# Attention units of a four-layer graph kernel: six of eight cover one head over all nodes instead of two heads over half of them

## The chip, the core and the metric

The kernel runs on one core of one Trainium2 chip. The core has a matrix engine (TensorE, PE in the profile; its weight loads are shown as PEld), a vector engine (VectorE, DVE), a scalar engine (ScalarE, ACT), a general engine (GpSimd, POOL) and SyncE (SP), which issues most of the DMA transfers; POOL and ACT issue some as well. Each engine works through its own list of instructions in order and waits for others by semaphores. SBUF is the on-chip memory of 128 partitions, PSUM the memory that PE writes to. The metric is the device time of one execution in microseconds (us); lower is better.

## What is computed

A graph of N = 3327 nodes has features x (3327 x 512) and a 0/1 adjacency. Four layers follow one another, each x = layernorm(x + layer(x)). Layers 0 and 2 are graph attention with 8 heads of 64 features, layer 3 with 4 heads of 128, layer 1 takes the mean over the first 64 neighbours of a node. Cut to what matters here:

```
# layers 0 and 2: H = 8 heads, D = 64 (layer 3: 4 heads, D = 128)
Wh = x @ W                          # (N, H, D)
f1, f2 = Wh . a1, Wh . a2           # one number a node and head each
e  = leaky_relu(f1[i] + f2[j], 0.2)
e  = where(adj[i, j] > 0, e, -9e15)
att = softmax(e, over j)
h[i] = sum_j att[i, j] * Wh[j]      # layer 2 and 3: then elu
# layer 1
keep = first 64 neighbours of each row
x = leaky_relu(mean(keep) @ W_nb.T + b_nb) + leaky_relu(x @ W_line.T + b_line)
```

## The kernel before

**Tiles.** The nodes are padded to NP = 3328 = 26 tiles of 128 (NT = 26). A half is 13 tiles, IW = 1664 nodes. The mask (adjacency, transposed: neighbours j on the partitions, nodes i along the row) is held as bytes (fp8).

**A unit of attention.** `attention` (L598) runs eight units, `for half in range(2): for s in range(NS)`, and `unit` (L370) does one: a slot s, which is two heads (HS = 2) in layers 0 and 2 and one head in layer 3, for one half of the nodes i. Its loop `for j in range(NT)` (L419) goes over the 26 tiles of neighbours. For each j and each head, `weights` (L408) issues one instruction on DVE, L411, which makes the masked weight `t` (128 x 1664, f32) from the broadcast row `rb` of that head, a column `qc` and the mask, and one on ACT, L414, which makes `y`, its share below the kink of the leaky relu, as bytes. PE multiplies `t` by the values `vj` into four PSUM banks `po` (L434); the two heads of 64 features stand side by side in the array. An f32 matmul shows as two instructions, so one j is 16 `po` matmuls. The sums of the denominator go to `pd` (L386) in `den` (L383): 8 matmuls a j with `y` and the columns `sden`, and 8 with the mask and the columns `sm`. `den` is called for a pair of j at a time, two to three j late (L437); the `sm` part of a pair belongs to one of the four slots of a half (L396), which add to the same `pd`.

**Buffers.** `t` has 6 buffers of one head and half, `y` 7 (layer 0) or 8, `vj` 4 of two tiles of 128 features, `rb` 3 rows (2 in layer 3). The rows of a unit are loaded by `rows` (L361) on POOL's queue when a buffer is free; they come out of the DRAM tensor `rd`, which `prepare` (L305) writes.

**Around the loop.** What else has to be done is put into two lists, `background` and `aside`, of which each j takes one job (L439 to L442). At a unit's end ACT copies `po` to `ob` (L454), PE transposes it in four jobs (L462) and SP stores it to `hd`. After the last unit of a half, the sums are finished: by 26 tiny matmuls and `reciprocals` (L561 to L579) after the first half, by DVE transposes and small transfers after the second.

**The mask.** `mask_steps` (L643) loads int32 pieces of the adjacency (`raw`, 128 x 832) and turns each to bytes on DVE (L640) or ACT (L639). The first half's 52 pieces come during the projection of layer 0, the second half's 52 in `aside` during units 0 and 1, one a j, with two `raw` buffers; half 1 of the nodes is first used in unit 4. `count_jobs` (L659) count neighbours, for one half in unit 0, for the other in unit 2. In unit 3 the mask is stored to DRAM (`md`). For layers 2 and 3 `MaskTiles` (L692) loads it back in pieces of a tile and a half: 8 tiles of the first half late in layer 1 on POOL's queue, the others in units 0 and 1 of layer 2 on SP's.

**Order.** PE's order is that of the program; the order of the other engines is decided by a scheduler when the kernel is built, except for instructions that `keep_in_program_order` pins (among them the mask pieces of layer 0's units). `prepare` for the first half is called in layer 0 during its projection (L1186), in layer 1 in one go after tile 12 has been projected (`job2`, L928), where PE works at the sums L908; for the second half it is a job of unit 0.

Of the kernel before, what the change touches and what calls it, by code (L numbers as in the profile page):

```python
# [32 lines left out]
def kernel(  # L33
# [198 lines left out]
    class Layer:  # L232
# [72 lines left out]
        def prepare(self, pool, half, tag="rr", bufs=2, pinned=False):  # L305
# [4 lines left out]
            ins = nc.vector.tensor_scalar(rc, rc, RCLAMP, -RCLAMP, op0=ALU.min, op1=ALU.max)  # L310
            if pinned:
                tc.keep_in_program_order(ins)
            nc.scalar.activation(rc, rc, AF.Exp, scale=ALPHA - 1.0)
            for s0, n in QUADS:
                t0 = half * HALF + s0
                pr = qp.tile([P, 4 * P], F32, name="pr", tag="q")
                for s in range(n):
# [4 lines left out]
            nc.scalar.activation(qc, qc, AF.Exp, scale=1.0 - ALPHA)  # L322

            nc.vector.tensor_scalar(sc.bitcast(I32), qc.bitcast(I32), 0x7F800000, None,
                                    op0=ALU.bitwise_and)
            nc.vector.reciprocal(sc, sc)
            nc.vector.tensor_scalar(sc, sc, STEP, None, op0=ALU.mult)
            nc.vector.scalar_tensor_tensor(bi, qc, -1.0, sc, op0=ALU.mult, op1=ALU.mult)
# [32 lines left out]
        def rows(self, rp, half, s):  # L361
            rb = []
            for h in range(s * self.HS, (s + 1) * self.HS):
                r_ = rp.tile([P, IW], F32, name="rb")
                nc.gpsimd.dma_start(out=r_, in_=self.rd[h:h + 1, half * IW:(half + 1) * IW].to_broadcast([P, IW]))  # L365
                rb.append(r_)
            return rb


# [251 lines left out]
    QW = IW // 2  # L621

    def mask_load(pool, t, q, eng):
# [8 lines left out]
    def mask_set(raw, t, q, on_act=False):  # L632
# [26 lines left out]
    def count_jobs(pool, half):  # L659
        jobs = []  # L660
        for s0, n in QUADS:
# [12 lines left out]
            def none(i0=i0, w_=w_, held=held):  # L674
                ct = pool.tile([P, 4 * P], BF, name="ct", bufs=1)
# [5 lines left out]
                nb = pool.tile([P, 4 * P], F8, name="nb", bufs=1)  # L681
# [10 lines left out]
    class MaskTiles:  # L692
        FIRST = 8
# [5 lines left out]
        def start(self):  # L699
            self.early = self.pools.enter_context(tc.tile_pool(name="mk_a", bufs=1, side="right", reuse_waits="tile"))  # L700

        def load(self, pool, j, half, eng=nc.sync):
            m = pool.tile([P, IW], F8, name=f"mk{half}_{j}")
            ins = eng.dma_start(out=m, in_=md[j * P:(j + 1) * P, half * IW:(half + 1) * IW])
            if eng is nc.sync:
                tc.keep_in_program_order(ins)
            self.tiles[j, half] = m
# [582 lines left out]
```

## Time and profile before

| | us |
|---|---|
| median of 3 runs | 3255.55 (3254.47 to 3257.07) |
| the profiled execution | 3259.11 |
| its span | 3257.0 |
| PE busy | 3137.8 (96%) |
| DVE busy | 2654.7 (82%) |
| ACT busy | 2349.7 (72%) |
| granted PE clock, mean | 0.984 |

Layer 0 projects until some 134 us and its units run until 957; layer 1 runs to some 1600; the units of layer 2 go from 1631 to 2424, and layer 3 ends at 3257. The costliest groups of the page are `po` (L434: 8320 instructions, 1913.4 us), `y` on ACT (L414: 1040, 1770.1) and `t` on DVE (L411: 624 with the mask tiles `mk`, 1180.7, and 416 with `mask`, 779.9).

Busy times on PE are modelled at their ends: a busy PE need not be at its peak. "Idle before" is what the engine waited for just ahead of an instruction. The chain of waits follows the work that ended last back from the end of the program; each of its lines has the start, the length, the engine, the tensor, the line and how many instructions are merged.

### The profile page before, as it was taken

Reading aid. Unit: us, or ns where it says so; the run is one execution under the profiler, and the core shown is the slowest. Engines: PE = TensorE matmul, PEld = TensorE weight load, DVE = VectorE, ACT = ScalarE, POOL = GpSimd, SP = SyncE. Lnnn points to the kernel's source line nnn. Section 1 sums busy time; section 2 is a strip of 40 time slices with the busy share of each in tenths; the row PEclk is TensorE's granted clock in tenths of the full one; section 3 lists DMA queues with packets and bytes.
Section 4 is the critical chain, followed back from the end, with each engine's and each line's share of the span. In section 5 each row is a group of like instructions: output and inputs, shape, how many; then the busy total and the mean of one; then the engine's idle time right before and its main releaser. Section 6 shows DMA issues by size and latency. Waiting matters only on the chain.

```text
span 3257.0 us, 45993 instructions
## 1 busy us (share of the span) xinstructions
PE 3137.8 (96%) x17802; PEld 1670.4 (51%) x17802; DVE 2654.7 (82%) x2581; ACT 2349.7 (72%) x2131; POOL 242.6 (7%) x397
## 2 busy tenths in 40 slices
PE   8899999999999999999989999999998999999997
PEld 7644444444444467767734444444447654445443
DVE  5699999999977645545499999999989666678986
ACT  1398999999973334444389999999988655559976
POOL 3100000000001011111100000000011000010110
PEclk9999999999999999999999999999999999999998
DMA  9445314111124345545412211111127211122211
GB/s 372 158 129 162 102 56 159 46 50 50 46 85 152 102 125 133 140 121 131 133 49 76 82 53 47 36 49 50 43 90 246 90 43 43 42 52 89 94 39 50
DMA packets 337289, 310.63 MB, mean 95 GB/s; under 512 B 154084, under 2 KB 269102, under 8 KB 337071
## 3 DMA queue, kind: packets, MB, share of 16 engines
q1 hardware_dynamic: 302831, 195.34, 20.1%
q0 software_dynamic: 28720, 104.67, 10.1%
q10 hardware_dynamic: 5520, 7.69, 0.7%
q8 instruction: 141, 2.31, 0.3%
q14 instruction: 77, 0.63, 0.1%
HBM read 230.75 MB, written 76.84 MB: 94 GB/s over the span
## 4 chain that ended last, share of the span: by engine, by line
PE 84%; DVE 6%; DMA 4%; ACT 3%; issue 2%; SPq 0%; POOL 0%; ACTq 0%; DVEq 0%; POOLq 0%
PE po L434 53%; PE acc L908 9%; PE pd L386 7%; PE pw L277 5%; DVE t L411 3%; PE pz L807 2%; PE pi L810 2%; DMA raw<-in_adjT_dram 2%; ACT y L414 2%; PE pk L778 1%; PE pt L462 1%; DMA h<-hd 1%; PE pa L1161 0%; DVE xr L197 0%; DVE st L153 0%
## 5 line engine op out<-in xcount | busy, mean ns | idle before, releaser
L414 ACT ACTIVATE y<-t,bi,sc 128x1664 fp8e4<-128x1664 f32 x1040 | 1770.1, 1766 | 308.7 <-PE pd L386 290.6
L434 PE MATMUL po<-t,vj 128*64 128x448 f32 (+3 forms) x8320 | 1913.4, 521 | 23.5 <-DVE t L411 21.2
L434 PEld LDWEIGHTS po<-t,vj 128*64 128x64 f32 (+1 forms) x8320 | 837.9, 148 | 976.2 <-issue 706.9
L411 DVE SCALAR_TENSOR_TENSOR t<-rb,qc,mk 128x1664 f32<-128x1664 f32 x624 | 1180.7, 1939 | 165.6 <-PE po L434 148.8
L411 DVE SCALAR_TENSOR_TENSOR t<-rb,qc,mask 128x1664 f32<-128x1664 f32 x416 | 779.9, 1945 | 8.8 <-PE po L434 5.7
L908 PE MATMUL acc<-zs,kt 128*128 128x512 f32 x1352 | 361.1, 421 | 0.0
L277 PE MATMUL pw<-wsb,xT 128*128 128x264 f32 (+1 forms) x1248 | 299.7, 395 | 10.8 <-ACT xT L268 3.5
L908 PEld LDWEIGHTS acc<-zs,kt 128*128 128x128 f32 x1352 | 257.4, 190 | 52.7 <-PE pk L760 0.8
L386 PE MATMUL pd<-y,sden 128*32 128x448 fp8e4 (+1 forms) x4160 | 259.5, 341 | 11.0 <-ACT y L414 11.0
L767 ACT CAST pk<-cy 128x512 f32<-128x512 bf16 x169 | 99.3, 588 | 236.2 <-DVE kt L781 229.7
L277 PEld LDWEIGHTS pw<-wsb,xT 128*128 128x128 f32 x1248 | 239.7, 196 | 53.5 <-ACT xT L268 8.2
L781 DVE SCALAR_TENSOR_TENSOR kt<-pk,mb 128x512 fp32r<-128x512 f32 x169 | 115.6, 684 | 125.0 <-PE pk L778 123.9
L386 PEld LDWEIGHTS <-sden 128*32 128x32 bf16 x4160 | 117.3, 96 | 163.6 <-issue 140.7
L365 POOL DMA_DIRECT2D rb<-r x40 | 21.5, 537 | 1643.4 <-DVE t L411 1525.7
L283 DVE TENSOR_TENSOR vt<-pw,dc 128x256 f32<-128x256 f32 x156 | 58.8, 416 | 91.3 <-ACT dc L278 87.5
L737 POOL DMA_DIRECT2D cy<-ctd x91 | 68.0, 748 | 392.1 <-ACT pk L767 301.5
L807 PE MATMUL pz<-wn,xT 128*128 128x512 f32 x208 | 95.0, 600 | 0.6 <-ACT xT L801 0.5
L810 PE MATMUL pi<-wl,xT 128*128 128x512 f32 x208 | 93.6, 592 | 0.0
L155 ACT ACT_TABLE_LOAD x46 | 59.0, 1283 | 41.7 <-DVE mv L154 41.1
L182 DVE TENSOR_TENSOR h<-h,rec 128x512 f32<-128x512 f32 x65 | 43.7, 683 | 54.7 <-DMA h<-hd 54.6
L281 ACT COPY rc<-pw 128x8 f32<-128x8 f32 (+1 forms) x78 | 12.7, 162 | 89.3 <-PE pw L277 86.6
L640 DVE TENSOR_SCALAR mask<-raw 128x832 fp8e4<-128x832 int32 (+3 forms) x81 | 49.2, 615 | 25.5 <-DMA raw<-in_adjT_dram 25.4
(185 smaller groups left out, 1650.5 us busy)
## 6 DMA issues: line engine op xcount, KB each, us to landing
vj<-v SPq DMA_DIRECT2D x312, 128.0 KB
rb<-r POOLq DMA_DIRECT2D x40, 832.0 KB, 4.8
raw<-in_adjT_dram SPq DMA_DIRECT2D x67, 416.0 KB
cy<-ctd POOLq DMA_DIRECT2D x78, 256.0 KB, 4.1
h<-hd SPq DMA_DIRECT2D x61, 256.0 KB
v<-vt SPq DMA_DIRECT2D x50, 256.0 KB
hd<-hb SPq DMA_DIRECT2D x48, 256.0 KB
xr<-x POOLq DMA_DIRECT2D x45, 256.0 KB, 3.1
```

What stands on the lines that cost most here:

```text
L155: nc.scalar.activation(rs[:, :n, 0], mv[:, :n, 1], AF.Sqrt, bias=eps)
L277: nc.tensor.matmul(pw[e][:, :FW + H], xT[:, c, :], wsb[:, c, e, :], start=c == 0, stop=c == FC - 1)
L386: nc.tensor.matmul(pd[c][32 * kk:32 * kk + 32, :w_], lhsT, rhs, start=(kk, c) not in seen, skip_group_check=final is not None, stop=last a ...
L411: nc.vector.scalar_tensor_tensor(t, rb[k], self.qc[:, j, h:h + 1], mask_at[0](j, i0, IW), op0=ALU.max, op1=ALU.mult)
L414: nc.scalar.activation(y, t, AF.Sigmoid, bias=self.bi[:, j, h:h + 1], scale=self.sc[:, j, h:h + 1], saturate=False)
L434: nc.tensor.matmul(po[c][k * D:(k + 1) * D, :z - a_], vj[:, j % 2, k * D:(k + 1) * D], ts[k][:, a_:z], start=j == 0, stop=j == NT - 1)
L737: nc.gpsimd.dma_start(out=cy[:, :n, :], in_=ctd[t:t + n, b * GW:(b + 1) * GW] .rearrange("(o t) i -> o t i", o=1).to_broadcast([P, n, GW]))
L767: nc.scalar.copy(pks[k % 2], carry[b, t // 4 * 4][:, t % 4:t % 4 + 2, :])
L781: nc.vector.scalar_tensor_tensor(kt, pk, NEIGHBOURS, mb[:, t:t + 2, :], op0=ALU.is_le, op1=ALU.mult)
L807: nc.tensor.matmul(pz, xT[:, c, :], wn[:, c, :], start=c == 0, stop=c == FC - 1)
L810: nc.tensor.matmul(pi, xT[:, c, :], wl[:, c, :], start=c == 0, stop=c == FC - 1)
L908: nc.tensor.matmul(acc, kts[b, t][:, s * P:(s + 1) * P], zs(t, c), start=t == 0 and c == 0, stop=t == NT - 1 and c == 1)
```

## The change

Layers 0 and 2 get units of their own (`unit8`, `attention8`). Layer 3 keeps `unit`. The eight units are now: unit 0, heads 0 and 1 over the first half ("narrow", as before); six "wide" units, of one head each over all 3328 nodes, in two groups of three (heads 2, 4, 6, then 3, 5, 7); unit 7, heads 0 and 1 over the second half. A wide unit makes `t` and `y` of a j with one instruction each over 3328 elements; PE's matmuls have the shapes they had, with the two halves where the two heads were. Each group has its own `pd`.

```diff
+    UNITS = [Unit(0, 0, 1, half=0, head=0)] + \
+        [Unit(1 + par, n, 3, head=2 * slot + par) for par in range(2) for n, slot in enumerate((1, 2, 3))] + \
+        [Unit(3, 0, 1, half=1, head=0)]
...
+        def den(j, y):
...
+            order = [(c, k, e) for c in range(2) for k in range(2) for e in range(2)]
+            if j % u.of == u.pos:
+                for c, k, e in order:
+                    a_, w_ = part(c, e)
+                    x_ = 32 * u.section(k)
+                    go(c, k, e, self.sm[:, j, x_:x_ + 32], mask_at[0](j, u.base(k) + a_, w_), w_, False)
+            for c, k, e in order:
+                a_, w_ = part(c, e)
+                x_ = 88 * u.section(k) + PIECES[u.slot] - 8 * u.slot
+                go(c, k, e, self.sden[:, j, x_:x_ + 32], y[:, k, a_:a_ + w_], w_, u.last)
+
+        def weights(j, t, y, k):
+            if u.wide:
+                h, to, yo, ro, m = u.h, *(a.rearrange("p k i -> p (k i)") for a in (t, y, rb)), mask_at[0](j, 0, NP)
+            else:
+                h, to, yo, ro, m = u.h + k, t[:, k, :], y[:, k, :], rb[:, k, :], mask_at[0](j, u.base(k), IW)
+            nc.vector.scalar_tensor_tensor(to, ro, self.qc[:, j, h:h + 1], m, op0=ALU.max, op1=ALU.mult)
+            nc.scalar.activation(yo, to, AF.Sigmoid, bias=self.bi[:, j, h:h + 1],
+                                 scale=self.sc[:, j, h:h + 1], saturate=False)
...
+            for c, (a_, z) in enumerate(CUTS):
+                for k in range(2):
+                    x_ = 0 if u.wide else k * D
+                    nc.tensor.matmul(po[c][k * D:(k + 1) * D, :z - a_], vj[:, j % 2, x_:x_ + D],
+                                     t[:, k, a_:z], start=j == 0, stop=j == NT - 1)
+            late.append((j, y))
+            while len(late) > 1 + (n == 0 and j < 2):
+                den(*late.pop(0))
...
+            for k in range(2 if u.wide else 1):
+                w_ = D if u.wide else 2 * D
+                r0 = u.base(k) + s0 * P
+                nc.sync.dma_start(out=hd[r0:r0 + n_ * P, f0:f0 + w_].rearrange("(t p) f -> p t f", p=P),
+                                  in_=hb[:, :n_, k * w_:(k + 1) * w_])
...
+        with tc.tile_pool(name="at_t", bufs=3, reuse_waits="tile") as tp, \
+                tc.tile_pool(name="at_y", bufs=3, reuse_waits="tile") as yp, \
+                tc.tile_pool(name="at_v", bufs=3, reuse_waits="tile") as vp, \
```

The buffers of `t` and `y` now hold a j for both halves or heads, three of each. The row of a unit has a ring of two buffers of 3328 (`wide_rows`), one of which stays on for layer 3, whose rows use its two halves. The sums of the first three groups are finished by the tiny matmuls, those of unit 7 by DVE and transfers.

Because unit 1 needs the mask of all nodes, the second half comes earlier and in smaller pieces, and its count follows in unit 1 instead of 2; the attention vectors of layers 2 and 3 are projected in unit 2 instead of 1. In layer 2 the mask tiles of both halves are loaded in unit 0.

```diff
-        pieces = pieces[EARLY:]
+        pieces = [(t, q, IW // 4) for t in range(NT) for q in range(4, 8)]
+        rest = ExitStack()
+        rawp = rest.enter_context(tc.tile_pool(name="raw", bufs=3))
+        ring.insert(0, (rest.enter_context(tc.tile_pool(name="at_s0", bufs=1, reuse_waits="tile")), "rbb"))
+        msteps = mask_steps(rawp, pieces, 2, [k for k in range(len(pieces)) if k % 9 in (1, 3, 5, 7)], True)
+
+        def some(n):
+            for f in msteps[n:n + 3]:
+                f()
...
+                def reload(j):
+                    if j + mask_tiles.FIRST < NT:
+                        mask_tiles.load(j + mask_tiles.FIRST, 0)
+                    mask_tiles.load(j, 1)
```

`MaskTiles.FIRST` goes from 8 to 3. `prepare` is cut into six steps, and layer 1 runs one of them at tile 14 of each following row of sums, instead of all at once:

```diff
+            return [clamp] + [lambda s0=s0, n=n: quad(s0, n) for s0, n in QUADS] + [scales]
...
+                            if side and t == 14:
+                                side.pop(0)()
...
-                                nxt.prepare(sp, 0, "xi", 1)
+                                side.extend(nxt.prepare_steps(sp, 0, "xT", 1))
...
                     if b == len(blocks) - 2:
-                        mask_tiles.load_first()
+                        for j in range(mask_tiles.FIRST):
+                            mask_tiles.load(j, 0, nc.gpsimd)
+                        nxt.first_rows = nxt.wide_rows(ring, UNITS[0])
```

## The prediction

> **What bounds the kernel now.** I read the busy time by stage first, then the chain of waits inside one attention unit, then the timeline of VectorE (DVE) there, and last the chain around `prepare` in layer 1. The columns of the first view are: stretch, its length, then busy us of PE, PEld, DVE, ACT and POOL with their instruction counts, granted clock, DMA share, GB/s.
>
> ```profile
> 751.00:848.00 97.00, 95.50 (x685) 40.50 (x685) 97.00 (x53) 90.33 (x61) 1.06 (x2) 1.00 0.14 45
> ```
>
> This is one unit of layer 0. DVE is busy in all of it, PE in 98%, at full clock. Both look like the bound, so the chain inside the unit has to tell.
>
> ```profile
> 780.54 2.94 PE po L434 x16
> 783.49 0.59 PE pt L462 x4
> 784.07 2.94 PE po L434 x16
> 787.02 1.62 PE pd L386 x27
> 788.64 2.94 PE po L434 x16
> 791.58 0.26 PE pt L462
> 791.84 2.94 PE po L434 x16
> 794.79 0.87 PE pd L386 x14
> 795.65 5.74 PE po L434 x32
> 801.39 0.87 PE pd L386 x14
> 802.26 6.34 PE po L434 x32
> ```
>
> One `po` block is one tile j: 2.94 us when other work stands on both sides, 5.74 for two in a row. A `pd` block of 16 matmuls takes 0.87, of 32 (16 more with `sm`) 1.62, so 16 `sm` matmuls cost 0.75. From 802.26 on the same 32 `po` matmuls take 6.34 and then 6.58: PE has caught up and waits inside the block for `t`. The DVE timeline has the pace of `t`:
>
> ```profile
> 788.70 18.70 DVE L411 SCALAR_TENSOR_TENSOR t<-rb,qc,mask 128x1664 f32<-128x1664 f32 x10
> ```
>
> One instruction lasts 1.94, so the step from one to the next is (18.70 - 1.94)/9 = 1.862 us, and 52 of them make 96.8 us. PE's own work in a unit is 13 x (5.74 + 0.87) + 13/4 x 0.75 + three blocks of transposes of 0.59, one of 0.26 and their breaks 0.5 = 90.8. The markers of the chain at 468.08, 565.69, 663.82, 760.27 and 857.13 put a unit at 97.3: DVE sets the pace, PE has 6 us to spare, ACT 7.
>
> **The wide instruction.** Two rows give DVE's price per element.
>
> ```profile
> L283 DVE TENSOR_TENSOR vt<-pw,dc 128x256 f32<-128x256 f32 x156 | 58.8, 416 | 91.3 <-ACT dc L278 87.5
> L182 DVE TENSOR_TENSOR h<-h,rec 128x512 f32<-128x512 f32 x65 | 43.7, 683 | 54.7 <-DMA h<-hd 54.6
> ```
>
> (683 - 416)/256 = 1.043 ns an element, so 1664 elements are 1.735 us and 0.127 of the step is fixed. A wide instruction takes 3.470 + 0.127 = 3.597 instead of 3.724, and a wide unit 26 x 3.597 = 93.5 of DVE. No row has 3328 elements: it costs at most two old steps (3.724) and at least the elements alone (3.470); I take 3.597. ACT falls too and has room.
>
> **What PE gets in exchange.** `den` runs after each j, no longer after each pair: 26 blocks of 8 matmuls and 26 `po` blocks of 2.94. Layer 3 has such a block of 8 in its chain (two records are missing from the count):
>
> ```profile
> 2877.64 0.49 PE pd L386 x6
> ```
>
> The `sm` matmuls were shared out over the four units of a half, 16 for each fourth pair. Now a group has one unit (narrow) or three (wide), so a narrow unit issues 8 for every j (0.375) and a wide one for every third: over a layer 832 instead of 416. PE's own time:
> narrow 26 x (2.94 + 0.49 + 0.375) + 2.0 = 100.9; wide 26 x 3.43 + 26/3 x 0.375 + 2.0 = 94.4.
> So PE becomes the bound in both: a wide unit is worth 97.3 - 94.4 = 2.9 at best, and a narrow one loses 4. Because PE and DVE (93.5) lie within 1% of each other and the tiles are uneven (3.43 or 3.81), I add 0.7 of waits to each unit: 95.1 and 101.6. The bounds are 0 and the whole 2.9. At a unit's end PE waited for the last `y` (1.76 at 757.92); now one `den` of 8 waits and DVE runs ahead, so I charge nothing more; without that lead it would be 1.8 a unit.
>
> **Side work, no longer hidden.** While DVE set the pace, PE's 6 us hid the counts (four of 1.62 + 0.32 = 7.8 a half), the projection of the attention vectors (8 x 1.0) and the sums (26 tiny matmuls, 1.6). Where PE is the bound they count.
>
> Layer 0, from the first `t` (134.27) to the last `pd` (956.76), 822.5 before. Unit 0 stays with DVE: 96.8 + the mask pieces + 3.8 of counts + 5.4 for cutting the columns of the other half + 2 of starting waits. The second half of the mask is now needed in unit 1, so it comes in 104 pieces of 416 columns, three a j: 76 of them in unit 0, 42 on DVE. An 832-column piece steps in 0.50; a half one lies between 0.25 and 0.50; with the fixed 0.127 it is 0.31, so 13.0. Unit 0: 121.0. PE's 100.9 + 7.8 + 3 hide beneath it. Units 1 to 7: 95.1 + 7.8 + 1.6 = 104.5; 95.1 + 8.0 = 103.1; 95.1; 95.1 + 1.6 = 96.7; 95.1; 95.1; 101.6 + 1.6 = 103.2. With 3.6 for the first wide `t` that PE must await and 0.5 for the last `den`: 817.9, a gain of 4.6.
>
> Layer 2: PE is the bound from 1671.3 on, with 20 tiles of unit 0 left: 20 x 3.81 + 0.5 = 76.7, then 96.7, 95.1, 95.1, 96.7, 95.1, 95.1, 103.2: it ends at 2425.0 against 2424.0 (2422.24 + 1.79), a loss of 1.0. The mask tiles come two a j on SP's queue instead of one; they are asked for three tiles ahead, some 11 us, and the 208 KB are less than the raw piece below, so nothing. The 26 loads of the second half stood in unit 1's list before; they are moved, not added.
>
> **The mask pieces' loads.** Three buffers, and a load waits for the third piece before it. Behind a waiting load stand the `vj` loads on SP's queue, which have three pairs of lead, and behind a late piece, pinned in DVE's order, the next `t`. In the old stretch:
>
> ```profile
> 263.66 4.20 DMA raw<-in_adjT_dram
> 970.20 1.94 DMA mb<-md
> ```
>
> 416 KB took 4.20 and 64 KB 1.94, so 208 KB should land in about 2.9. The ring turns in 2.9 + 0.35 (issue) + 0.31 (set) + 0.9 until the engine's turn (half a step of `t`) = 4.5, and a j of unit 0 has 121/26 = 4.65. That is hardly enough; I charge 4 us. Lower bound 0, or -3 if the wait on the last old piece (7.86 at 357.22) is no longer there; upper bound with 4.20 for the half piece: (5.76 - 4.65) x 35 = 39.
>
> The wide units' `vj` and `hd` rows are 256 bytes instead of 512. The `mb` transfer above is 64 KB in rows of 256 bytes, as a wide `vj` is: 1.94, with 7.2 us for each and three buffers, so nothing. The Trainium skill (DMA: Bandwidth & Descriptors, Specifications) speaks against the change here: below 512 bytes a transfer loses line rate. By that rule a wide `vj` would take as long as a narrow one with twice the bytes; it would still be hidden, and the sum would stay as it is.
>
> **Rows prepared in six places** (layer 1, bounded by PE).
>
> ```profile
> 1404.57 1.28 ACT L313
> ...
> 1410.83 1.82 DMA r<-rr
> ...
> 1413.37 0.38 PE pr L318
> 1413.75 3.41 PE acc L908 x8
> ```
>
> PE leaves its projection at 1404.37 and is back at its sums at 1413.75: 9.4 us, in which 13 transposes do 2.0 of work. They waited for the table load and Exp, for `qc` and for one buffer `rr` whose store came late. Split over six rows of tiles (35 us apart) each store is long done: 7.4 gained (bounds 0 and 9.4). The `rr` now shares the buffer of `xT`, free between tiles 9 and 21 when the step runs at 14; were it not, PE would wait for a 1.8 us store.
>
> The rest (rows in a ring of two, one `e` buffer at the layer's end, layer 3's rows in one tile) moves transfers that were issued 92 us early; 0, bounds -1 and +2.
>
> **Sum:** -4.6 + 1.0 + 4 - 7.4 = -7.0. The profiled execution has a span of 3257.0 (3259.11 in all); the median of the runs is 3255.55. 3255.55 - 7.0 = 3248.5.
>
> **Rivals.**
> 1. No waits: PE's bare sums hold (0.7 less in 14 units, 9.8) and the pieces come in time (4): 3234.7. For it: PE ran exactly at 2.94 and 0.87 from 760 to 802. Against it: DVE is only 1% below. Chance 0.20.
> 2. Slower: unit 0 waits for raw pieces. It decides from a landing above 3.0 us. At 3.8 the ring takes 5.36, 0.71 more than a j has, over 35 j 25 us instead of 4: 3269.5. For it: three pieces of 213,000 bytes in 4.65 are 137 GB/s, on top of the rest, where one of 426,000 came in some 4.0. Against it: 256 KB of `xr` land in 2.9 by the median of its issues. Chance 0.20.
> 3. The wide instruction saves nothing (3.724): DVE holds a wide unit at 96.8 + 0.7, 2.4 more in 12 units: 3277. Against it: the two rows above. Chance 0.10.
> 4. Slower: splitting `pd` costs more than 0.49 a block. At 0.60, 0.11 x 26 x 14 = 40: 3288; it decides from 0.51. Against it: the block of 8 in layer 3. Chance 0.07.
>
> **How the numbers follow.** The forecast has 0.43, its own range 3238 to 3258. What a measurement can tell from no change is about 0.2%, 6.5 us. Faster: rival 1 and a little over half of the forecast, 0.43; same: most of the rest and the mild ends of 2 and 3, 0.20; slower 0.37. The range goes from 3228 (rival 1 with the whole 9.4 in layer 1, the old last-piece wait gone, 3, and the rest at -1) to 3282 (past rival 3, short of rival 4).
>
> **What would show it.** In a wide unit `t` steps in 3.60 and the span of a unit is 94.4 to 96, with DVE showing idle time that `po` ends; in a narrow one about 101, with `sm` in every `den`. If `po` still shows blocks stretched by `t`, DVE is still the bound. Idle time of DVE before a mask piece, ended by the raw load, would be rival 2. No idle time of PE before `pr` in layer 1 would confirm the 7.4. The forecast is wrong if wide units stay at 97 or unit 0 takes over 130.

## The result and the profile after

The changed kernel takes 3267.74 us (median of 7 runs, 3263.78 to 3275.56) against 3255.38 for the kernel before: a ratio of 1.0039, with a 95% interval of 1.0027 to 1.0051. It is slower, by 9 to 17 us. The forecast was 3248.5, faster by 7. The profiled execution took 3265.22 with a span of 3263.5; that is 2.5 below its median, and the profiled execution of before was 3.7 above its own, so the two traces differ by 6.5 us only. Stage by stage (each mark is the start of the first, or the end of the last, instruction named):

| stage | before | after | difference | predicted |
|---|---|---|---|---|
| start to last `pd` of layer 0 | 956.9 | 958.0 | +1.1 | -0.6 (-4.6 and +4 for raw pieces) |
| to first `po` of layer 2 | 675.9 | 668.9 | -7.0 | -7.4 |
| to last `pd` of layer 2 | 791.3 | 794.8 | +3.5 | +1.0 |
| to first `po` of layer 3 (its projection) | 134.4 | 141.9 | +7.5 | 0 |
| to the end | 698.6 | 699.9 | +1.3 | 0 |

First the wide units, by the busy time in one of them, unit 5 of layer 0 (columns: stretch, its length, then busy us of PE, PEld, DVE, ACT and POOL with counts, granted clock, DMA share, GB/s):

```profile
663.00:757.70 94.70, 94.70 (x723) 35.16 (x716) 93.82 (x27) 85.13 (x36) 1.05 (x2) 1.00 0.13 37
```

94.7 instead of 97.3, PE now busy in all of it and DVE a little less. The timeline of PE inside unit 4 (start, length, engine, line, operation, count) shows why:

```profile
571.43 3.01 PE L717 MATMUL po<-t,vj 128*64 128x448 f32 x16
574.37 0.56 PE L675 MATMUL pd<-y,sden 128*32 128x448 fp8e4 x8
574.86 3.01 PE L717 MATMUL po<-t,vj 128*64 128x448 f32 x16
577.80 0.56 PE L675 MATMUL pd<-y,sden 128*32 128x448 fp8e4 x8
578.29 3.01 PE L717 MATMUL po<-t,vj 128*64 128x448 f32 x16
581.24 0.56 PE L675 MATMUL pd<-mask,sm 128*32 128x448 fp8e4 x8
581.58 0.60 PE L675 MATMUL pd<-y,sden 128*32 128x384 fp8e4 x8
582.11 3.01 PE L717 MATMUL po<-t,vj 128*64 128x448 f32 x16
```

From one `po` to the next it is 3.43 (574.86 - 571.43), and 3.82 where `sm` comes between (582.11 - 578.29). No line of this stretch has idle time in front. The timeline of DVE in the same unit has thirteen wide instructions in a row:

```profile
557.42 46.83 DVE L695 SCALAR_TENSOR_TENSOR t<-rba,qc,mask 128x3328 f32<-128x3328 f32 x13
```

One lasts 3.68, so a step is (46.83 - 3.68)/12 = 3.596. In layer 1, PE's timeline has the row transposes, now in four of the six places, some 17.7 us apart, with no wait in front of any:

```profile
1425.69 0.60 PE L324 MATMUL pr<-ident,rc 128*8 128x128 f32 x4
1443.46 0.60 PE L324 MATMUL pr<-ident,rc 128*8 128x128 f32 x4
1460.99 0.60 PE L324 MATMUL pr<-ident,rc 128*8 128x128 f32 x4
1478.75 0.28 PE L324 MATMUL pr<-ident,rc 128*8 128x128 f32 x1
```

Unit by unit, from the first `po` of a unit to the first of the next (of the last to its last `pd`), the six wide units of layer 2 are 14.9 us shorter together (570.1 against 585.0), and the two narrow ones 18.2 longer (118.7 and 105.9 against 108.7 and 97.7). Layer 0 has the same picture: 10.8 shorter and 13.7 longer.

One pair of traces is not enough to price these two layers. In the seven traces that have the new units with `den` at each j (this one and those of later runs, some with edits of buffers or of the mask's pieces), layer 2 took 794.8 to 802.0, in the four with the old units 788.7 to 791.3; layer 0 ended at 954.4 to 962.7 against 953.1 to 956.9.

The largest new loss is in layer 3's projection, where the rows of layer 3 are prepared in one go. PE's timeline there, before and after (in square brackets the idle time ahead of an instruction and what ended it):

```profile
2503.79 1.04 PE L318 MATMUL pr<-ident,rc 128*4 128x128 f32 x8 [0.90 <-ACT rc L281]
2506.04 0.75 PE L318 MATMUL pr<-ident,rc 128*4 128x128 f32 x5 [1.21 <-ACT rr L320]
...
2507.06 3.67 PE L277 MATMUL pw<-wsb,xT 128*128 128x260 f32 x16
```

```profile
2507.35 1.44 PE L324 MATMUL pr<-ident,rc 128*4 128x128 f32 x8 [4.31 <-ACT rc L318]
2509.63 1.37 PE L324 MATMUL pr<-ident,rc 128*4 128x128 f32 x5 [0.85 <-ACT rr L326]
...
2511.65 5.16 PE L277 MATMUL pw<-wsb,xT 128*128 128x260 f32 x16
```

Before these lines the changed kernel is 0.5 us ahead (a `pt` at 2494.29 against 2494.83); the `pt` behind them starts at 2516.65 against 2510.57, 6.1 late. ACT's timeline tells what came between:

```profile
2501.53 0.63 ACT L189 ACTIVATE e<-h 128x512 f32<-128x512 f32 x1 [1.06 <-DVE xr L197]
2503.49 0.25 ACT L313 ACTIVATE rc<-rc 128x52 f32<-128x52 f32 x1 [1.33 <-DVE rc L310]
...
2503.93 1.28 ACT L155 ACT_TABLE_LOAD   x1
```

```profile
2503.39 1.28 ACT L155 ACT_TABLE_LOAD   x1
2505.44 0.30 ACT L155 ACTIVATE rs<-mv,eps 128x2 f32<-128x2 f32 x1 [0.77 <-DVE mv L154]
2505.75 1.28 ACT L318 ACT_TABLE_LOAD   x1
2507.05 0.25 ACT L318 ACTIVATE rc<-rc 128x52 f32<-128x52 f32 x1
```

Before, the Exp of `rc` stood behind another Exp and ahead of the square root of the row norms, on a table that was there. After, it stands behind the square root: two table loads of 1.28, a wait of 0.77 and the square root itself come first, while PE stands. The Trainium skill (ScalarE: Activation LUTs, What ACT_TABLE_LOAD costs) gives 1283 ns for such a load, which the rows confirm. The rule of the same page (Table sets: the hidden batching unit), to batch functions by table set, is what the order before did here and the order after does not.

ACT's order is not the whole of it. The Exp needs the clamp of `rc`, which is an instruction of DVE, and DVE's timeline, before and after, has that late as well:

```profile
2503.27 0.18 DVE L310 TENSOR_SCALAR rc<-rc 128x52 f32<-128x52 f32 x1
```

```profile
2505.63 0.18 DVE L315 TENSOR_SCALAR rc<-rc 128x52 f32<-128x52 f32 x1
```

After, the finishing steps of two other tiles (L197, L198, L153, L154) stand in front of it, before it was the first two steps of one. With ACT's old order alone the Exp could have started when the clamp ends, at 2505.8 instead of 2507.05; with the early clamp alone it would still have stood behind the square root and the two table loads. Neither was tried by itself.

The wait also costs more than its own length. These are busy times in the changed kernel just before PE goes on, just after, and later (same columns as above; the third figure from the end is the granted clock):

```profile
2499.30:2507.30 8.00, 3.74 (x16) 2.92 (x16) 8.00 (x25) 5.15 (x11) 1.08 (x2) 1.00 0.62 199
2507.90:2514.60 6.70, 5.85 (x21) 3.96 (x19) 6.70 (x24) 6.00 (x11) 1.08 (x2) 0.50 0.60 195
2514.70:2521.00 6.30, 6.30 (x34) 5.48 (x33) 4.88 (x14) 5.32 (x11) 1.06 (x2) 1.00 0.64 189
```

For some 6.8 us the granted clock is 0.50. In that time the two `pr` lines take 1.44 and 1.37 instead of 1.04 and 0.75, the `pt` behind them 1.06 instead of 0.60 and the `pw` 5.16 instead of 3.67: 3.0 us. So the 6.6 us lost at this place are some 3.5 of waiting and 3.0 of PE at half its clock. In the kernel before the clock stays at 1.00 there, from 2503.7 to 2514. All five runs that have the wait of 4.3 (this one, four raw buffers, even pace, two `e` buffers, layer 2's units alone) have the 0.50 behind it. Layer 0's units alone, with a wait of 2.10, has it for 3.4 us; the run with layer 3's rows spread, with 0.36, has none.

### The profile page after: what moved, and what is told of

Read it like the earlier page. It is cut to its first block, busy times and chain, and to the rows that moved or that the text cites. A ratio compares the mean times of both kernels' runs of the same rounds, so it can differ in the third digit from the quotient of the medians.

```text
span 3263.5 us, 46836 instructions
## 1 busy us (share of the span) xinstructions
PE 3161.3 (97%) x18738; PEld 1598.6 (49%) x18738; DVE 2624.2 (80%) x2328; ACT 2299.9 (70%) x1859; POOL 235.4 (7%) x384
## 5 line engine op out<-in xcount | busy, mean ns | idle before, releaser
L696 ACT ACTIVATE y<-t,bi,sc 128x3328 fp8e4<-128x3328 f32 (+1 forms) x520 | 1342.7, 2604 | 144.6 <-PE pd L675 91.2
L717 PE MATMUL po<-t,vj 128*64 128x448 f32 (+1 forms) x6656 | 1266.6, 522 | 15.4 <-DVE t L695 14.3
L717 PEld LDWEIGHTS po<-t,vj 128*64 128x64 f32 x6656 | 450.4, 137 | 699.4 <-issue 621.2
L451 PE MATMUL po<-t,vj 128*128 128x448 f32 (+1 forms) x1664 | 607.2, 518 | 1.4 <-DVE t L428 1.4
L428 DVE SCALAR_TENSOR_TENSOR t<-rba,qc,mk 128x1664 f32<-128x1664 f32 x208 | 404.1, 1949 | 163.8 <-PE po L451 145.9
L431 ACT ACTIVATE y<-t,bi,sc 128x1664 fp8e4<-128x1664 f32 x208 | 358.4, 1767 | 198.1 <-PE pd L403 190.3
L695 DVE SCALAR_TENSOR_TENSOR t<-rba,qc,mk 128x3328 f32<-128x3328 f32 (+1 forms) x130 | 379.8, 2987 | 11.2 <-DMA mk<-md 7.5
L695 DVE SCALAR_TENSOR_TENSOR t<-rba,qc,mask 128x3328 f32<-128x3328 f32 (+1 forms) x130 | 381.8, 2986 | 8.3 <-PE po L717 8.0
L695 DVE SCALAR_TENSOR_TENSOR t<-rbb,qc,mask 128x3328 f32<-128x3328 f32 (+1 forms) x130 | 381.5, 2985 | 6.6 <-PE po L717 4.1
L695 DVE SCALAR_TENSOR_TENSOR t<-rbb,qc,mk 128x3328 f32<-128x3328 f32 (+1 forms) x130 | 379.9, 2985 | 5.7 <-PE po L717 4.9
L277 PE MATMUL pw<-wsb,xT 128*128 128x264 f32 (+1 forms) x1248 | 305.0, 400 | 17.7 <-ACT xT L268 5.1
```

What stands on the lines that cost most here:

```text
L277: nc.tensor.matmul(pw[e][:, :FW + H], xT[:, c, :], wsb[:, c, e, :], start=c == 0, stop=c == FC - 1)
L428: nc.vector.scalar_tensor_tensor(t, rb[k], self.qc[:, j, h:h + 1], mask_at[0](j, i0, IW), op0=ALU.max, op1=ALU.mult)
L431: nc.scalar.activation(y, t, AF.Sigmoid, bias=self.bi[:, j, h:h + 1], scale=self.sc[:, j, h:h + 1], saturate=False)
L451: nc.tensor.matmul(po[c][k * D:(k + 1) * D, :z - a_], vj[:, j % 2, k * D:(k + 1) * D], ts[k][:, a_:z], start=j == 0, stop=j == NT - 1)
L695: nc.vector.scalar_tensor_tensor(to, ro, self.qc[:, j, h:h + 1], m, op0=ALU.max, op1=ALU.mult)
L696: nc.scalar.activation(yo, to, AF.Sigmoid, bias=self.bi[:, j, h:h + 1], scale=self.sc[:, j, h:h + 1], saturate=False)
```

## The experiments

Ratios are to the kernel before, run on the same chip in turn with each. Where a stage of a run is told, it is a stage of the table above, in that run's profiled execution.

**Six places alone.** The kernel before with this edit:

```diff
-                                nxt.prepare(sp, 0, "xi", 1)
+                                side.extend(nxt.prepare_steps(sp, 0, "xT", 1))
...
+                            if side and t == 14:
+                                side.pop(0)()
```

> The kernel before with the rows of layer 2 prepared in six places, and nothing else of the change. Theory: this part is worth the 7.3 us by which the first po of layer 2 came closer in the changed kernel (1632.76 against 1626.94, with layer 0 ending 1.1 to 1.5 later), so 3248, and layer 3's projection (last pd of layer 2 to first full block of po: 142.2 us) stays as it was. Rival: the loss of 7.6 us in layer 3's projection belongs to this part too, because it changes what the scheduler sees; then the time is that of the kernel before, 3255.

Measured: 3246.14 against 3254.24, 0.9974 (0.9964 to 0.9984). Layer 1 takes 668.8, layer 3's projection 135.5 (the 142.2 named above counts to a later mark, the first full block of `po`). The part is worth what was forecast, and the loss in layer 3 is not its doing: the rival falls.

**Layer 3's rows spread out.** The changed kernel with:

```diff
                         if t == HALF + 1:
-                            L3.prepare(pp, 0)
-                            L3.first_rows = L3.rows(rp, 0, 0)
-                            L3.cut(pp, 0)
+                            side = L3.prepare_steps(pp, 0)
+                        if t > HALF and side:
+                            side.pop(0)()
+                            if not side:
+                                L3.first_rows = L3.rows(rp, 0, 0)
+                                L3.cut(pp, 0)
```

> The changed kernel with layer 3's first rows also prepared in six places, one step a tile from tile 14 on. Theory: PE's wait of 4.31 for the Exp of rc, 0.85 for rr and the stretched block behind them (5.16 instead of 3.67) came from DVE and ACT reaching the clamp and the Exp late; spread out, 5 to 7 us go: 3262 by the median of 3267.7, and no pr waits over 1 us. Rival: the projection is slower because of the finishing steps (h loads, one e buffer) and PE meets the same delay at a pt instead: within 2 us of 3267.7.

Measured: 3256.81 against 3254.24, 1.0010 (1.0001 to 1.0019): of the 0.39% only 0.10% is left, some 9 us gone. The projection takes 135.3 instead of 141.9. PE's timeline of this run:

```profile
2505.13 0.60 PE L324 MATMUL pr<-ident,rc 128*4 128x128 f32 x4 [0.36 <-ACT rc L318]
2511.02 0.60 PE L324 MATMUL pr<-ident,rc 128*4 128x128 f32 x4
2515.40 0.60 PE L324 MATMUL pr<-ident,rc 128*4 128x128 f32 x4
2519.78 0.27 PE L324 MATMUL pr<-ident,rc 128*4 128x128 f32 x1
```

The wait of 4.31 is 0.36, and the granted clock stays at 1.00 behind it. That PE stood at the late Exp is shown: take the wait away, and the stage is back at its old length. ACT still has a square root and two table loads between one Exp and the next here; the steps only come early enough now. The edit gained more than the 5 to 7 expected of it by the medians, and just that (6.6) by the stage. What is left is 0.10% slower than before, where 0.2% faster was forecast for the change: the other half of the miss is not in this stage.

**`den` in pairs again.** `den` for two j at a time, first `sm` of both, then `y` of both:

```diff
-            while len(late) > 1 + (n == 0 and j < 2):
-                den(*late.pop(0))
+            if len(late) > 2:
+                both()
...
+        def both():
+            pair = [late.pop(0), late.pop(0)]
+            for sums in (True, False):
+                for j_, y_ in pair:
+                    den(j_, y_, sums)
```

> The changed kernel with den called for two j at a time again (sm of both, then y of both), y still in three buffers. Theory: a pair costs PE 5.74 + 0.87 instead of 2 x (2.94 + 0.49), 0.25 less, 3.25 a unit; a narrow unit that PE bounds gains all of it (unit 7 twice, 20 tiles of layer 2's unit 0: 9 us), a wide one only what lies above DVE's 93.5 (some 1 a unit, 12 us): 3267.7 - 20 = 3248. Rival: with three buffers ACT must wait for the den of the pair before the next y, and the 3.16 of a y leave no room (6.32 of 6.6 a pair): wide units at 97 or more, 3290.

Measured: 3240.00 against 3254.24, 0.9954 (0.9942 to 0.9966): faster than both kernels. Layer 0 ends at 945.1, 12.9 before the changed kernel, and units 3 to 6 take 91.3, 98.3, 91.3 and 93.3, on average 93.55. In the timeline of DVE in those units

```profile
557.14 50.42 DVE L695 SCALAR_TENSOR_TENSOR t<-rba,qc,mask 128x3328 f32<-128x3328 f32 x14
```

there is no gap: (50.42 - 3.68)/13 = 3.595 a step, 93.5 for 26. DVE sets the pace again, at the lower price of the wide instruction, and PE's extra jobs are hidden: the 98.3 has them, and the units at 91.3 catch up. So the wide units had been held by the split of `den`, as the forecast's PE sum says: the same four units took 97.1 on average before the change and 95.2 after it, so the split had given away about half of what the wide instruction can save there. The Trainium skill (TensorEngine Tiling (Array Packing), Key Properties) says that a change of the tiling mode drains TensorE, without a price. Here `po` works in tiles of 64 columns and `pd` in tiles of 32, and a pair takes 0.25 less than two single j: 2 x 3.43 against 6.61 in the rows of the forecast. That the drain is the reason is not shown: `po` and `pd` differ in type and shape too. The forecast for this run, 20 us, was passed by 8, and as much came from layer 3's projection, which took 134.0 instead of 141.9 though nothing was edited there. The narrow units did not gain as forecast: unit 0 took 124.6 in layer 0 and 122.0 in layer 2, instead of 119.3 and 118.7 (in layer 2 it waits for a mask tile, see below). Unit 7 of layer 2 took 110.0 instead of 102.6 from `ob` copies to `ob` copies, but these come 3.4 us before the last `pd` in the changed kernel and behind it here; to the last `pd` it is 109.4 against 105.9. Unit 7 of layer 0 is shorter, 105.1 against 107.6.

**Four raw buffers.** The changed kernel with `bufs=4` for `raw` and a lag of 3 instead of 2.

> The changed kernel with four raw buffers and the pieces set three behind their loads, not three and two. Theory: DVE's 8.4 us of waiting for raw pieces in units 0 and 1 (4.27 of it in one wait at 259.01, while the row of unit 2, 1664 KB, came in) fall by half or more, and units 0 and 1 end 4 to 7 us earlier: 3262. Rival: the pieces are late because the transfers share the engines (three pieces and a row at once), so that one more buffer only moves the wait: within 2 us of 3267.7.

Measured: 3270.95, 1.0047 (1.0035 to 1.0059). No gain. The waits in layer 0's first units (engine and line that waited, for what: us in total, times, longest), in the changed kernel and in this run:

```profile
ACT mask L869 <- DMA raw<-in_adjT_dram: 11.8, 14, 2.0
DVE mask L870 <- DMA raw<-in_adjT_dram: 8.4, 8, 4.3
```

```profile
DVE mask L870 <- DMA raw<-in_adjT_dram: 11.7, 10, 4.1
ACT mask L869 <- DMA raw<-in_adjT_dram: 5.9, 5, 1.6
ACT L869 <- DMA raw<-in_adjT_dram: 4.6, 1, 4.6
```

DVE's waits rose, and ACT's are 10.5 where they were 11.8. The theory of too few buffers falls.

**An even pace for the pieces.** Two or three pieces a j, and the counts of the second half in unit 2:

```diff
         def some(n):
-            for f in msteps[n:n + 3]:
-                f()
+            for f in msteps[:2 + n % 2 * (n < NT)]:
+                msteps.pop(0)()
...
-            if n == 1:
-                return count_jobs(pool, 1)
             if n == 2:
-                jobs = []
+                jobs = count_jobs(pool, 1)
```

> The changed kernel with the raw pieces spread evenly over units 0 and 1 (two and three a j in turn in unit 0, two a j in unit 1, instead of three a j), and with the counts of the second half in unit 2 instead of unit 1, since their mask tiles are later. Theory after the run with four buffers: the pieces are late because three of them a j, a vj and a row of 1664 KB ask for more than the DMA engines give; at 2.5 pieces a j, 114 GB/s instead of 137, DVE's 8.4 us of waits in layer 0 go to below 3 and units 0 to 2 together (335.7 us from 134 to 469.7) lose 4 to 6 us. Rival: the waits are the row's alone (4.27 of 8.4 at 259.01) and stay: less than 2 us.

Measured: 3268.72, 1.0035 (1.0022 to 1.0047), no gain. Units 0 to 2 end at 471.1 (changed kernel 469.7); unit 1 is shorter by 3.0 and unit 2, which has the counts now, longer by 3.6. DVE waits 10.5 for the pieces. So the demand for bytes isn't the cause either, as the theory had it. The rival, that the waits are the row's alone and stay, fits, but the row was not moved; which of row, `vj` and queue delays the pieces stays open. Most of unit 0's length is work: in the changed kernel DVE is busy in 117.7 of the 120 us from 134, and 6.4 of its 8.4 us of waits lie in unit 1.

**Two `e` buffers.** The changed kernel, finishing layer 2's first tiles with two buffers `e` as before; to make room, the rows of its second half share a buffer:

```diff
-                            [lambda: L2.prepare(mp, 1, "rr", 1, True), lambda: L2.cut(mp, 1, "pc", 1, True)]
+                            [lambda: L2.prepare(mp, 1, "pc", 1, True), lambda: L2.cut(mp, 1, "pc", 1, True)]
...
-                           ending=lambda sp: ends.extend(finish(f2, x2, L2, 0, 2, 2, nc.sync, None, sp, 1)))
+                           ending=lambda sp: ends.extend(finish(f2, x2, L2, 0, 2, 2, nc.sync, None, sp, 2)))
```

> The changed kernel with two buffers e for the finishing of layer 2's first two tiles, as before the change (to make room, the rows of layer 2's second half share a buffer with the cut columns). Theory: the one e buffer only shifts the first 30 us of layer 3's projection, which the wait for the weights hides; the loss sits at the rows of layer 3, so the projection stays at 141 to 142 us, the time within 2 of 3267.7. Rival: the single e is what throws the order out; then the projection falls to 134 to 136 and the time to 3261.

Measured: 3269.70, 1.0043 (1.0031 to 1.0056), the projection 141.5, with the same 4.31 in front of `pr`. The rival falls. Layer 2 took 802.0 in this run's trace, 7 more than in the changed kernel; whether the shared buffer costs that was not looked into.

**Pairs in the wide units alone.** In narrow units `den` stays at one j:

```diff
+            if u.wide:
+                if len(late) > 2:
+                    both()
+            else:
+                while len(late) > 1 + (n == 0 and j < 2):
+                    one()
```

> The changed kernel with den called for two j at a time in the wide units only. Theory: in the run with pairs everywhere the narrow units lost what the wide ones gained (unit 7 of layer 2 took 110.0 against 102.6, unit 0 of layer 0 ended 5.5 later), because two y instructions a j and a held pair do not fit three buffers; the wide ones fell to 91.3 to 93.5. With both at their better form: 3240 - 5 - 2 - 7 = 3226. Rival: the wide units' gain comes from being started later (they catch up), then 3240 or more.

Measured: 3245.64 against 3255.49, 0.9964 (0.9951 to 0.9976). Faster than both kernels, but not 3226. Layer 2 takes 788.9 against 793.7 with pairs everywhere, layer 0 ends later, 952.4 against 945.1, and unit 7 of layer 2 is still at 108.3. The theory was wrong about layer 0. About layer 2 it was right by sign in this pair of traces, but the granted clock of that stage was 0.99 here and 0.98 there, which over 790 us can be most of the 4.8. Layer 3's projection takes 134.2, again with no edit in it or in unit 7 in front of it. The wait for the Exp is 0.36. ACT's timeline there has the square root at 2489.18, a table load at 2489.49 and the Exp at 2490.79: the same order as in the changed kernel, and yet the Exp comes in time, since DVE's clamp is done at 2488.8. So ACT's order alone does not make the wait.

**Both rows spread out, without the new units.** The kernel before with the edits of the first two experiments:

> The kernel before with the rows prepared in six places in layer 1 and in six tiles of layer 3's projection. Theory: what PE loses there in the kernel before is 0.90 + 1.21 in front of pr and little else, so 1 to 3 us less than the kernel with layer 1's six places alone: 3244. Rival: a step a tile disturbs the finishing steps of the tiles, no gain: 3246 or more.

Measured: 3246.50, 0.9976 (0.9965 to 0.9986), no different from layer 1 alone (0.9974). The projection took 135.0. The rival holds: where the Exp comes early, spreading those rows gives nothing.

**Layer 3's weights first.** The changed kernel with layer 3's rows spread, and:

```diff
+                load_wide(wsb, w3, nc.gpsimd)
                 load_group(2)
-                load_wide(wsb, w3, nc.gpsimd)
```

> The changed kernel with layer 3's rows in six places, and with the load of layer 3's weights issued on POOL's queue ahead of the first two tiles' h and xr instead of behind them. Theory: PE's wait of 4.02 for wsb at the start of the projection goes to about 1, but h comes 1.5 later and the waits for ACT's h (2.81 and 4.74 in the run with six places) take its place, so the projection stays between 133 and 136: 3256. Rival: the start of the projection is a chain that begins with the weights, and 3 us come off: 131 to 133, 3253.

Measured: 3256.79 against 3252.62, 1.0017 (1.0009 to 1.0026); the projection takes 135.6. PE's timeline:

```profile
2422.68 0.68 PE L277 MATMUL pw<-wsb,xT 128*128 128x260 f32 x2 [1.79 <-DMA wsb<-in_w_dram]
2425.59 8.51 PE L277 MATMUL pw<-wsb,xT 128*128 128x260 f32 x30 [2.23 <-DMA wsb<-in_w_dram]
2443.94 1.97 PE L267 MATMUL pt<-ident,h 128*128 128x128 f32 x8 [9.84 <-ACT h L162]
```

The two waits for the weights are 4.0 together instead of 4.36 (4.02 and 0.34), and the next two waits for `h` are 9.84 and 1.06 where they were 2.81 and 4.74. What the weights gave, the next tiles of `h` took: the rival's 3 us are not there.

**Pairs with more `y` buffers.** Pairs everywhere, rows of layer 3 spread, its weights first; four `y` in layer 2, then also in layer 0 at the price of one `vj`:

```diff
-                tc.tile_pool(name="at_y", bufs=3, reuse_waits="tile") as yp, \
+                tc.tile_pool(name="at_y", bufs=3 + (self.li == 2), reuse_waits="tile") as yp, \
```

> The changed kernel with den in pairs in all units, four y buffers in layer 2 (room from shared buffers: the rows of its second half with the cut columns, red with hb), three in layer 0, layer 3's rows in six places and its weights first. Theory: against the run with pairs and three y (3240.0), unit 7 of layer 2 falls from 110 to 98 to 102, since y no longer waits for a held pair, and unit 0 by 2 to 5; layer 3's projection stays at 133 to 135: 3226 to 3230. Rival: the narrow units are held by something else (DVE, the two y a j on ACT); then 3238 or more.

> The same with four y buffers in layer 0 too, for which vj has two buffers in both layers instead of three. Theory: layer 0's unit 7 falls from 105.8 to 99 to 101 and unit 0 ends at 254 instead of 259, 3218 to 3224. Rival: with two vj buffers the load behind a waiting raw piece comes late in units 0 and 1, and layer 0 gains nothing: 3228 or more.

Measured: 3246.05 (0.9977, 0.9968 to 0.9985) and 3251.23 (0.9990, 0.9979 to 1.0001). Both miss, on the side of their rivals. Layer 2 takes 793.8 and 793.6, as with three. Unit 7 of layer 2 does fall to 103.3, but the wide units go from 92.4 to 93.5 and from 97.0 to 99.6 (one of layer 2's stretches ran at a clock of 0.93). Layer 3's projection, which has its own edits here, takes 137.9 and 134.5. For the layer as a whole the fourth `y` buys nothing. A narrow pair costs DVE 4 x 1.862 = 7.45 and PE 5.74 + 0.75 + 0.87 = 7.36: pairs take PE (7.61 for two single j) off the bound there and meet DVE at once, which the forecast of 3.25 a unit in the third experiment had missed.

**Layer 0's units alone, layer 2's units alone.** The first keeps layers 2 and 3 of the kernel before, the second its layer 0; both have the six places in layer 1.

> The new units in layer 0 alone, with layer 1's rows in six places; layers 2 and 3 as before the change. Theory: the stages add. Layer 0 costs 1 to 3 us, layer 1 gives 7.3, layer 2 stays at 790.8, and layer 3's projection at 134 to 136, since its order is set behind layer 2: 3255.5 + 2 - 7.3 = 3250. Rival: layer 3's projection is thrown out by anything that shifts what comes before; then 141 to 142 there and 3257.

> The new units in layer 2 alone (with the masks and the rows of layer 3 that belong to them) and layer 1's rows in six places; layer 0 as before the change. Theory: layer 0 ends at 953 to 957, layer 1 gives 7.3, layer 2 takes 3.5 more, layer 3's projection 7.5 more and its rest 1.3 more: 3255.5 - 7.3 + 12.3 = 3260. Rival: without the new units in layer 0 the order at layer 3's rows is the old one: 3253.

Measured: 3254.27 (0.9995, 0.9985 to 1.0005) and 3260.58 (1.0009, 1.0000 to 1.0018). PE at layer 3's rows, first with layer 0's units alone, then with layer 2's:

```profile
2492.63 1.04 PE L324 MATMUL pr<-ident,rc 128*4 128x128 f32 x8 [2.10 <-ACT rc L281]
2494.88 1.23 PE L324 MATMUL pr<-ident,rc 128*4 128x128 f32 x5 [1.21 <-ACT rr L326]
```

```profile
2505.88 1.32 PE L324 MATMUL pr<-ident,rc 128*4 128x128 f32 x8 [4.30 <-ACT rc L318]
2508.16 1.37 PE L324 MATMUL pr<-ident,rc 128*4 128x128 f32 x5 [0.96 <-ACT rr L326]
```

The projection takes 135.6 and 142.2, as both theories had it. The late Exp comes with layer 2's new units and not with layer 0's. Against the kernel with six places alone (0.9974), layer 0's units cost 0.21%, some 7 us by the runs (4.3 at the end of layer 0 in the profiled executions) where 1 to 3 were expected, and layer 2's 0.35%, some 11. With the six places at -0.26% that makes +0.30%; measured was +0.39 (0.27 to 0.51). The parts add up.

**Pairs everywhere in layer 0, in wide units in layer 2.**

> The changed kernel with den in pairs in all units of layer 0, and in layer 2 in the wide units alone. Theory: the stages of the two runs with pairs add: layer 0 to 945 as in the one, layer 2 in 789 as in the other instead of 793.7, so 5 less than 3240.0: 3235. Rival: layer 2's length depends on when its mask tiles come, which moves with layer 0's end, and the 5 us are lost again: 3240.

Measured: 3241.98 against 3256.41, 0.9952 (0.9938 to 0.9967): the same as pairs everywhere (0.9954), so the 5 us of the theory are not there. Layer 0 ends at 946.2 as it should, but layer 2 takes 791.2 instead of 789, with unit 7 at 109.9. These two are the fastest versions found, about 0.5% under the kernel before and 0.85% under the changed one.

## Why the prediction was wrong

*The wide instruction.* 3.597 was forecast, 3.596 measured. Rival 3 falls.

*PE as the new bound.* 3.43 and 3.81 a tile were forecast, 3.43 and 3.82 measured. Wide units without side work took 94.6, 94.7 and 92.7 against 94.4 and 95.1 with the 0.7 of waits. There were no such waits in them: rival 1 was right in this term, and what the other terms lost is larger by some 8 us.

*Side work.* The sums were put at 1.6. PE's timeline of the changed kernel, at unit 7 of layer 0 and at unit 7 of layer 2:

```profile
862.83 3.08 PE L780 MATMUL pe<-c,db 128*128 128x16 f32 x26
865.83 4.71 PE L717 MATMUL po<-t,vj 128*64 128x448 f32 x16
...
2328.21 3.08 PE L780 MATMUL pe<-c,db 128*128 128x16 f32 x26
2331.21 3.01 PE L717 MATMUL po<-t,vj 128*64 128x448 f32 x16
```

They take 3.08 (the 26 are 13 f32 matmuls of two instructions each). The trace of before has the same 3.08 for its own sums, at 610.84, so 1.6 was too little from the start. Three units of each layer have them: 1.48 too little, six times, is 8.9 us. The block of `po` behind them takes 4.71 in the first case and its usual 3.01 in the second. The difference is the granted clock: 0.50 from 866.1 to 869.4, and 1.00 from 2331.2 to 2335. It falls like this behind two of the six sums of the changed kernel, and behind none of the two before. Unit 7 of layer 0 came out at 106.6 where 103.2 was forecast, and these two, 1.48 and 1.7, make most of it.

*The mask pieces.* 4 us were charged for the loads; DVE waited 8.4. That there would be such waits was right, their size half of it; that the ring of three buffers makes them was not, since a fourth buffer left them. The end of unit 1, 134.27 + 121.0 + 104.5 + 4 = 363.8 by the forecast, came at 365.8. Rival 2 (25 us) falls. The wide units' `vj` in rows of 256 bytes stayed hidden, as forecast: the changed kernel has no wait for one.

*Layer 0 as a whole* was forecast at -0.6 and cost +1.1 by the profiled pair, and more, some 7, by the runs with it alone. *Layer 2* was forecast at +1.0 and cost 3.5 by the profiled pair, which is the least that any two of the traces above give. Its unit 0 is the larger part: from the first `po` to the `ob` copies it took 118.1, where the 38.5 of the old start, the 76.7 and the 0.5 make 115.7. The start came near the old one, although PE now waits 3.23 for `sm` in it: the seventh tile begins 39.5 after the first `po`, 1.0 later than the forecast has it. Of the 20 tiles behind, the first takes 5.0 instead of 3.82, and the last, to the next unit's start, 5.6. At the first of them the forecast has a wait wrong. It put the mask tiles, asked for three tiles ahead, at "so nothing"; SP's queue and DVE's timeline have

```profile
1653.02 8.09 SPq L327 DMA_DIRECT2D r<-rr  x4
1661.16 0.82 SPq L940 DMA_DIRECT2D mk<-md  x2
1663.73 16.85 DVE L695 SCALAR_TENSOR_TENSOR t<-rba,qc,mk 128x1664 f32<-128x1664 f32 x9 [7.49 <-DMA mk<-md]
```

The loads of two mask tiles stand behind the stores of the rows, and DVE waits 7.49 for them. All twelve traces with the new units in layer 2 have one such wait, of 7.2 to 12.2, the four with the old units none. In the changed kernel it costs PE about 1 us (0.21 in front of a block of `po`, and that tile of 5.0); with pairs everywhere PE waits 3.92 and 0.90 for `t` there. An earlier load was not tried.

*Six places* were forecast at 7.4; 7.0 by the stage, 8.1 by the run. Confirmed, though the six rows of tiles lie some 17.7 us apart and not 35.

**The step that failed** most is the last one, "The rest (rows in a ring of two, one `e` buffer at the layer's end, layer 3's rows in one tile) moves transfers that were issued 92 us early; 0, bounds -1 and +2." It asked which transfers are moved and found them early enough. It did not ask what happens to the order of DVE and ACT, which a scheduler makes, in a stage where PE waits for both: layer 3's projection lost 7.5 us, more than the whole forecast gain: a wait of 4.31 instead of 0.90 for the Exp of `rc`, and the stretch at half the clock behind it. Spreading the rows brought 6.6 of them back. The trace of before had the warning: PE waited 0.90 there already, for an Exp that ACT started as soon as the clamp ended (2503.49 and 2503.45), with a table load of 1.28 right behind it.

That step is about half of the miss: 7.5 of 13.5 us by the profiled pair, some 9 of 19 by the runs. The other half lies mostly in layers 0 and 2. Known of it are two terms that were mis-sized, the sums (8.9 us, which the waits that did not come, some 8, make up for) and layer 2's unit 0 (2.4, with a wait for mask tiles that was put at nothing). By the runs, layer 0 costs some 7 where -0.6 was forecast; what makes the rest of that stays open.

What stays open: why the order on DVE and ACT changes with layer 2's units. It is not `e`, and it does not need an edit near by: with `den` in pairs in the wide units alone, behind the same unit 7, the clamp comes early again (0.36 in front of `pr`). The 1.3 us in the rest of layer 3 is within what other runs show for that stage (697.8 to 700.2).

*Rival 4* falls: a block of 8 does cost the 0.49 of the forecast. That price, which the forecast took as given, was all the same the one to save: undoing the split is worth 0.85% with the better order that came along (12.9 us in layer 0, where no order of layer 3 can mix in).

## What to carry to other kernels

Where a scheduler orders the engines, a change can lose its gain in a stage that it doesn't touch. Look in the trace for places where PE waits only briefly because a chain over two engines (here a clamp on DVE, then an Exp on ACT) ends just in time, and spread or pin them. Look at both engines of the chain: here each was late by itself. Count what comes behind a wait of PE too, since the granted clock can be down there. When a cheaper instruction takes the bound off one engine, look at what the other engine paid for it in the same edit: here the wide instruction saved DVE 3%, and splitting `den` gave about half of that back in the wide units; with pairs kept, the gain is there. Take the price of a small job, like the sums, from its own row in the trace of before, and when loads are asked for later, look at what stands in front of them in their queue.

## What the runs showed of the hardware

26 matmul instructions of 16 columns took 3.08 us, 0.12 each, in both kernels. The granted clock showed two values, 1.00 and 0.50: behind waits of PE of 4.3 us it was 0.50 for some 6.8 us (five runs), behind one of 2.10 for 3.4 (layer 0's units alone), and one block of 16 `po` matmuls took 4.71 instead of 3.01 in such a stretch. The same `po` and `pd` matmuls took 3.43 a j when they changed places at every j (changed kernel) and 6.61 for two when they did so at every second (kernel before). A row of 1664 KB, broadcast to 128 partitions, landed 8.6 us after its issue, and the longest wait for a raw piece (4.27, ended at 259.01) fell into that transfer, issued at 250.87; that the one caused the other was not tried. In most series the longer executions have the lower granted clock: with layer 0's units alone, spans went from 3246.2 (0.989) to 3257.8 (0.985), though one of 3257.0 had 0.988. The profiled execution was the fastest of these twelve, so a stage table of one pair can miss several us of a difference.
